# One attention-plus-mixture-of-experts kernel: VectorE work spread over more steps, with quotients and residual adds traced behind the next maxima

## The chip, the cores and the metric

The kernel runs on one core of one Trainium2 chip. The metric is the device time in microseconds (us) of one execution, and the time of a kernel is the median of its runs. Engines are called as in the profile: PE is the matrix engine (PEld its weight loads), DVE is VectorE, ACT is ScalarE, POOL is GpSimd, SP is SyncE, which issues most DMAs.

## The reference

The input x has 8 batches of 512 rows of 128 numbers. One layer is computed, all in float32:

```
x = x + attention(layernorm(x))      # 16 heads of 8 columns, causal, softmax(q k^T / sqrt(8)) v, then Wo, bo
x = x + experts(layernorm(x))        # 8 experts, the best 2 of each row by a softmax gate:
                                     # sum over 2 of p * (relu(x w1 + b1) w2 + b2), F = 512
```

## The kernel before, in words

**A score is computed twice.** For every head, `shifts()` multiplies q and k (tiles `s`, query rows on the partitions) only to find the maximum of each row; DVE reads each 128x512 bank of PSUM with a `tensor_reduce` (line 642, tile `pm`). The negated maxima (`nm`, line 648) are split into two bf16 numbers (`nh`), transposed by PE (`nmTp`, line 588), copied by ACT (`nmT`) and written by a POOL DMA into two extra rows of `q2` (line 596). `attend()` then multiplies k and q again with these rows (tiles `st`, key rows on the partitions, lines 783 and 788), ACT takes the exponential (line 793, tile `pt`), and PE accumulates the product with v in one PSUM bank `po` (line 704). The tiles `s` and `st` share one pool of four PSUM banks (`ps_sc`), so PE can start the next score only when DVE (for `s`) or ACT (for `st`) has read the bank of four tiles before.

**After two groups of four heads** ACT copies `po` to `ob` (line 713), and `divide()` transposes it on PE (`oqp`, line 725), then DVE takes a reciprocal (`rd`, line 728) and multiplies twice (`on`, line 730). After the last group of a batch, `out_T()` transposes `on` on PE (`oTp`, line 748), ACT copies it (`oT`, line 750), `out_project()` multiplies by Wo (`pp`, line 756), and DVE adds x (line 760).

**Then a batch is routed.** `route()` computes the second layer norm (`layernorm`, named f0 to f7), the gate, the two best experts of each row and a slot for each, all in small DVE instructions; `dispatch()` follows after batches 1, 3, 5, 6 and 7 and decides which tiles of 128 slots are complete. `scatter()` writes the rows to DRAM with 8 indirect DMAs of POOL for each batch (line 1052). `experts()` gathers them (SP DMAs, `xg<-xs`, line 1215), turns them (`xgTp`, line 1246; `xgT`, line 1248), multiplies with w1 (`ph`, line 1287), adds the bias and clips (`hT`: two of the four 128x128 pieces on ACT, line 1294, and two on DVE, line 1296; in the tail after batch 7, three and one), multiplies with w2 (`py`, line 1146), adds b2 on DVE (`yo`, line 1150) and writes the rows back with an indirect DMA (`ys`, line 1184). `sums()` adds the two results of each row at the end (line 1365).

**The order is written by hand.** Each of these parts is a generator that yields due times, in units of one batch of attention; the lane with the earliest due time traces its next instructions. PE, ACT, DVE and SP execute exactly in the order of tracing (`ORDERED`), and so do those instructions of POOL that go through `G_ops` or `in_order`. An instruction that waits therefore holds all that stands behind it on its engine. `in_order` also ties each indirect DMA to the exponential traced last before it. Steps of `attend()` are called in `go_on()`: one product and one waiting step (`late`) at each of 24 places in a batch. In `route()`, `soon(n)` moves the due time on by n steps of 0.012 to 0.025 batch.

The first layer norm of batch b (named a0 to a7) is traced in `norms()` for b of 2 and more: statistics (lines 369 and 370) on DVE from b - 2.16, a reciprocal root on POOL, and the normalised rows `xn` with four DVE instructions (line 384) from b - 2.0. `project()` transposes them at b - 1.84 (`xnTp_a`, line 395) and multiplies with Wv (`pv`, line 567) at b - 0.85.

Of the kernel before, what the change touches and what calls it, by code (L numbers as in the profile page):

```python
# [18 lines left out]
P = 128  # L19
# [7 lines left out]
def preln_attn_moe(ctx: ExitStack, tc: tile.TileContext, x, wq, wk, wv, wo, bo,  # L27
# [337 lines left out]
    def layernorm(src, name, t, each):  # L365
        stats = small.tile([P, NT, 6], F32, tag="stats", name=f"stats_{name}")
        mv = small.tile([P, NT, 2], F32, tag="mv", name=f"mv_{name}")
        for c in range(NT):
            nc.vector.bn_stats(stats[:, c, :], src[:, c, :])
            nc.vector.bn_aggr(mv[:, c, :], stats[:, c, :])  # L370
            yield t[0] + each * (c + 1)
        rstd = small.tile([P, NT], F32, tag="rstd", name=f"rstd_{name}")
        ve = small.tile([P, NT], F32, tag="ve", name=f"ve_{name}")
        first = name in ("a0", "a1")
        on_pool = nc.gpsimd if first else G_ops
        on_pool.tensor_tensor(ve, mv[:, :, 1], eps, ALU.add)
        on_pool.tensor_tensor(rstd, ve, mhalf, ALU.pow)
        yield t[1]
        xn = work.tile(
            [P, NT, D if name[0] == "a" else XROW], F32, tag=f"xn{name[0]}", name=f"xn_{name}",  # L380
            bufs=1 if name[0] == "a" else XB,
        )
        for c in range(NT):
            nc.vector.tensor_scalar(  # L384
                xn[:, c, :D], src[:, c, :], mv[:, c, 0:1], rstd[:, c : c + 1],
                ALU.subtract, ALU.mult,
            )
            if c < NT - 1:
                yield t[1] + each * (c + 1)
        return xn  # L390
# [11 lines left out]

    def norms():
        for b in range(2, B):
            yield b - 2.16
            normal[b] = yield from layernorm(xt[b], f"a{b}", (b - 2.16, b - 2.0), 0.025)


    packed, shifted, attended, added = set(), set(), set(), set()


    def project():
# [17 lines left out]
        for b in range(B):  # L430
# [7 lines left out]
                xn = normal.pop(b)  # L438
            if 0 < b < B - 2:
                xt[b + 2] = load_x(b + 2)  # L440
            yield b - (1.84 if b > 1 else 1.21 if b == 1 else 1.41)
            xnT = rows_T(xn, f"a{b}")
            late = 0.19 if b == 1 else 0.0
            yield b - (1.40 if early else 1.36) - early + late
# [115 lines left out]
                pack(0, 1)  # L560
                pack(1, 1)
            packed.add(b)
            yield b - 0.85
            assert b < 2 or b - 2 in added
            pv = mm_tile(f"pv_{b}")
            for c in range(NT):
# [16 lines left out]
    def shifts():  # L583
        late = []

        def transposed(b, g, nh):
            pt = mm_tile(f"nmTp_{b}_{g}").bitcast(BF16)
            nc.tensor.transpose(pt[:, :P], nh, ident_bf)
            nmT = small.tile([32, P], BF16, tag="nmT", name=f"nmT_{b}_{g}")
            nc.scalar.copy(nmT, pt[:32, :P])  # L590
            late.append(lambda: rows(b, g, nmT))

        def rows(b, g, nmT):

            for l in range(2):
                ins = nc.gpsimd.dma_start(  # L596
                    out=q2_buf[b % 2][KS + l : KS + l + 1, HG * g : HG * g + HG],
                    in_=nmT[16 * l : 16 * l + 16],
                )
                if b > 0:  # L600
                    tc.keep_in_program_order(ins)
            shifted.add((b, g, 2))

        for b in range(B):
            for g in range(G):
                t0 = b - LEAD + g / G + (0.1 if b == 0 < g else 0.0)
                yield t0
                assert b in packed
                q2, k2 = q2_buf[b % 2], k2_buf[b % 2]

                pm = pm_buf[g % 2].rearrange("p (n u) t k -> p u n (t k)", u=2)
                for pr in range(2):
                    n = 2 * g + pr
                    for i, unit in enumerate(S_UNITS):
                        yield t0 + (3 * pr + i) / 24
                        for v, bank in enumerate(unit):
                            ps = ps_sc.tile(
                                [P, T], F32, tag="sc", name=f"s_{b}_{n}_{i}_{v}"
                            )
                            for u, t, at in bank:  # L620
                                h, q = 2 * n + u, ts(t, P)
                                if t > 0:
                                    nc.tensor.matmul(  # L623
                                        ps[:, at : at + t * P], lhsT=q2[:KS, h, q],
                                        rhs=k2[:KS, h, : t * P],
                                        start=(at == 0), stop=True, skip_group_check=True,
                                    )
                                nc.tensor.matmul(  # L628
                                    ps[:, at + t * P : at + (t + 1) * P],
                                    lhsT=q2[:, h, q], rhs=k2[:, h, q],  # L630
                                    start=(at + t == 0), stop=True, skip_group_check=True,
                                )
                            blocks = ps.rearrange("p (a q) -> p a q", q=P)
                            if i == 0:
                                top, src = pm[:, v, pr, 12:13], ps
                            elif i == 1:
                                top, src = pm[:, v, pr, 3:7], blocks
                            else:
                                top, src = pm[:, :, pr, 8], ps.rearrange(
                                    "p (u k) -> p u k", u=2  # L640
                                )
                            nc.vector.tensor_reduce(top, src, AX.X, ALU.max)  # L642
                        if t0 + (3 * pr + i) / 24 < 0:
                            keep_warm(WARM[2], f"{g}_{pr}_{i}")
                        if late:
                            late.pop(0)()
                nm = small.tile([P, HG * NT], F32, tag="nm", name=f"nm_{b}_{g}")
                nc.vector.tensor_reduce(  # L648
                    nm, pm_buf[g % 2].rearrange("p h t k -> p (h t) k"), AX.X, ALU.max,
                    negate=True,  # L650
                )
                nh = nh_buf[g % 2]
                nm = nm.rearrange("p (h o a) -> p h o a", o=2, a=2)
                hi, lo = (
                    nh[:, ts(l, HG * NT)].rearrange("p (h a o) -> p h o a", a=2, o=2)
                    for l in range(2)
                )
                on_pool = V if b == 0 else G_ops
                on_pool.tensor_copy(hi, nm)
                on_pool.tensor_tensor(lo, nm, hi, ALU.subtract)  # L660
                if b > 0:
                    late.append(lambda: None)
                late.append(lambda b=b, g=g, nh=nh: transposed(b, g, nh))
                if b == 0 and g == 0:
                    for n in range(2):
                        yield t0 + (6 + n) / 24
                        late.pop(0)()
        while late:
            late.pop(0)()
            yield B - LEAD + 0.05  # L670


    def attend():
# [46 lines left out]
        def divide(b, ob, g):  # L720
# [4 lines left out]
                nc.tensor.transpose(pt[:, ts(t, P)], ob[:, ts(t, P)], ident)  # L725
            oq = pt.rearrange("p (k r) -> p k r", r=32)
            rd = small.tile([P, NT * HG, 2], F32, tag="rd", name=f"rd_{b}_{g}")
            nc.vector.reciprocal(rd, oq[:, :, HD : 2 * VC : VC])
            for o in range(2):
                nc.vector.tensor_tensor(  # L730
                    on[b][:, :, ts(g // 2, D // 2)].rearrange(
                        "p t (h o d) -> p t h o d", o=2, d=HD
                    )[:, :, :, o],
                    pt.rearrange("p (t h r) -> p t h r", t=NT, h=HG)[
                        :, :, :, VC * o : VC * o + HD
                    ],
                    rd[:, :, o].rearrange("p (t h) -> p t h", t=NT).unsqueeze(3).to_broadcast(
                        [P, NT, HG, HD]
                    ),
                    ALU.mult,  # L740
                )
            if g == G - 1:
                late.append(lambda: out_T(b))

# [8 lines left out]
        def out_project(b, oT):  # L753
            pp = mm_tile(f"pp_{b}")
            for t in range(NT):
# [1 line left out]
                    pp[:, ts(t, P)], lhsT=oT[:, ts(t, P)], rhs=wo_sb, start=True,  # L757
                    stop=True,
                )
            nc.vector.tensor_tensor(  # L760
                xt[b], pp.rearrange("p (c d) -> p c d", c=NT), xt[b], ALU.add
            )

        for b in range(B):
            for g in range(G):
# [46 lines left out]
    def route():  # L812
        for b in range(B):
# [8 lines left out]
                return now[0]  # L822

            yield now[0]
            t = [soon(0), soon(7), soon(4 if b == B - 1 else 6)]
            xn2[b] = yield from layernorm(
                xt[b], f"f{b}", t, step / 2 if b == B - 1 else step
            )
# [113 lines left out]
            lanes.append([now[0], 100 + b, scatter(k, b, now[0])])  # L942
            for s, (_, after, _, _) in enumerate(STEPS):
                if after == b:
                    yield from dispatch(s, soon)


    def dispatch(s, soon):
# [134 lines left out]
    def experts():  # L1083
# [192 lines left out]
        for n, (s, i) in enumerate(tiles):  # L1276
# [9 lines left out]
            for c in range(FC):  # L1286
# [1 line left out]
                    ph[:, ts(c, P)], lhsT=wt[s, i][:, ts(c, P)],  # L1288
                    rhs=turned[s, first][:, ts(i - first, P)], start=True, stop=True,
                )  # L1290
            for c in range(FC):
                bias = wt[s, i][:, F + c : F + c + 1]
                if c < (FC - 1 if after(s, i) else FC // 2):
                    nc.scalar.activation(hT[:, c, :], ph[:, ts(c, P)], AF.Relu, bias=bias)  # L1294
# [129 lines left out]
```

## Time and profile before

| what | value |
|---|---|
| time, median of 3 runs | 583.0 us (582.61 to 583.82) |
| the profiled execution's own time | 580.48 us |
| its span, first to last instruction | 578.8 us |
| mean granted TensorE clock | 0.966 |
| busy: PE, DVE, ACT, POOL | 506.7, 410.5, 307.3, 242.4 us |
| attention, 40 to 445 us: PE busy | 369.4 of 405 us |
| tail, 445 to 579 us: PE busy | 105.4 of 134 us |

The profiled execution is 2.5 us faster than the median of the runs, and 1.7 us of its time lie outside its span. Up to about 40 us the first batch is prepared; from there to about 445 us eight batches of attention follow at some 50.6 us each, and from 207 us on the experts' tiles run between them; then come the remaining tiles and the sums. A row of the waits reads: engine, tile and line that waited, who ended the wait, total us, number of times, longest us.

### The profile page before, as it was taken

What the parts mean: (1) busy time and instruction counts of PE and PEld (TensorE: products, weight loads), DVE (VectorE), ACT (ScalarE), POOL (GpSimd) and SP (SyncE); (2) the same over time, 40 slices, a digit from 0 to 9 for tenths busy, and PEclk for the clock granted to TensorE, in tenths of its full rate; (3) what the DMA queues carried; (4) which work ended last, traced back from release to release, by engine and by line L of the source; (5) the groups of instructions that cost most, each with busy time, mean ns of one, the idle gap of its engine ahead of it and who ended that gap; (6) DMA issues with size and microseconds to landing.
All of it is one profiled execution on the core that took longest, in us unless ns stands there. A gap on an engine that the chain in (4) does not pass through costs nothing. (4 is left out here: it accounts for less than half of the span.)

```text
span 578.8 us, 14044 instructions
## 1 busy us (share of the span) xinstructions
PE 506.7 (88%) x4762; PEld 373.9 (65%) x4762; DVE 410.5 (71%) x1272; ACT 307.3 (53%) x673; POOL 242.4 (42%) x380
## 2 busy tenths in 40 slices
PE   8868999988987989999899999998898889789980
PEld 6644556556544565665567777766576878689980
DVE  4987787887888779778978678787653445233694
ACT  3645666755754665575556555554564434245530
POOL 4032212405716423661753356345435524644442
PEclk9888899999998999999999999999999979989995
DMA  3728667288299572535526573222333686758783
GB/s 82 190 66 202 150 157 184 59 206 191 73 193 188 145 193 55 133 80 130 158 65 169 116 193 94 66 66 76 102 107 117 199 269 190 208 165 263 239 303 104
DMA packets 68761, 86.06 MB, mean 149 GB/s; under 512 B 11540, under 2 KB 50748, under 8 KB 66652
## 3 DMA queue, kind: packets, MB, share of 16 engines
q1 hardware_dynamic: 61508, 74.87, 50.0%
q0 software_dynamic: 6592, 9.65, 5.2%
q8 instruction: 39, 0.64, 0.5%
q10 hardware_dynamic: 592, 0.66, 0.5%
q14 instruction: 30, 0.25, 0.1%
HBM read 61.34 MB, written 26.16 MB: 151 GB/s over the span
## 5 line engine op out<-in xcount | busy, mean ns | idle before, releaser
L793 ACT ACTIVATE pt<-st 128x512 f32<-128x512 f32 x320 | 178.4, 599 | 109.0 <-PE st L783 49.3
L642 DVE TENSOR_REDUCE pm<-s 128x1 f32<-128x512 f32 (+2 forms) x320 | 205.5, 680 | 27.0 <-PE s L628 23.3
L1184 POOL DMA_INDIRECT ys<-yo,to x78 | 76.5, 980 | 99.1 <-ACT pt L793 32.4
L623 PE MATMUL s<-k,q 72*128 72x384 bf16 (+2 forms) x384 | 93.3, 278 | 15.8 <-ACT pt L793 9.9
L628 PE MATMUL s<-k,q 128*128 128x128 bf16 x512 | 94.1, 223 | 7.9 <-ACT pt L793 5.2
L783 PE MATMUL st<-q,k 128*128 128x128 bf16 x512 | 91.0, 220 | 10.2 <-DVE pm L642 5.5
L704 PE MATMUL po<-pt,va 128*18 128x512 f32 (+3 forms) x1024 | 91.6, 444 | 1.4 <-ACT pt L793 1.4
L788 PE MATMUL st<-q,k 74*128 74x256 bf16 (+2 forms) x384 | 91.9, 276 | 0.0
L1146 PE MATMUL py<-w_sb,hT 128*128 x624 | 87.4, 283 | 4.5 <-DVE have L962 2.2
L1146 PEld LDWEIGHTS py<-w_sb,hT 128*128 128x128 f32 x624 | 78.8, 197 | 7.8 <-issue 5.2
L1052 POOL DMA_INDIRECT xs<-xn_f,slot x64 | 64.0, 1000 | 30.9 <-ACT pt L793 15.6
L628 PEld LDWEIGHTS <-q 128*128 128x128 bf16 x512 | 50.9, 100 | 32.2 <-issue 29.2
L623 PEld LDWEIGHTS <-q 72*128 72x128 bf16 x384 | 37.6, 99 | 39.8 <-issue 32.2
L783 PEld LDWEIGHTS <-k 128*128 128x128 bf16 x512 | 50.9, 100 | 4.0
L788 PEld LDWEIGHTS <-k 74*128 74x128 bf16 x384 | 37.4, 98 | 22.7 <-issue 17.2
L596 POOL DMA_DIRECT2D q<-nmT x64 | 34.1, 536 | 39.5 <-ACT nmT L590 37.2
L358 POOL CAST nh<-nm 128x16 bf16<-128x16 f32 x28 | 5.6, 198 | 91.8 <-DVE nm L648 90.8
L1296 DVE TENSOR_SCALAR hT<-ph,wt 128x128 f32<-128x128 f32 x72 | 21.9, 346 | 28.8 <-ACT hT L1294 23.5
L704 PEld LDWEIGHTS po<-pt,va 128*18 128x18 f32 x1024 | 22.7, 96 | 30.1 <-issue 21.8
L1294 ACT ACTIVATE hT<-ph,wt 128x128 f32<-128x128 f32 x72 | 22.6, 364 | 35.7 <-issue 12.3
L1287 PE MATMUL ph<-xgT,wt 128*128 128x128 f32 x288 | 40.1, 282 | 0.7 <-issue 0.4
L1287 PEld LDWEIGHTS ph<-xgT,wt 128*128 128x128 f32 x288 | 35.0, 191 | 5.6 <-issue 2.7
(185 smaller groups left out, 697.6 us busy)
## 6 DMA issues: line engine op xcount, KB each, us to landing
wt<-wrows SPq DMA_DIRECT2D x36, 322.0 KB
k<-kparts SPq DMA_DIRECT2D x42, 192.0 KB
q<-wrows SPq DMA_DIRECT2D x24, 322.0 KB
k<-wrows SPq DMA_DIRECT2D x18, 322.0 KB
q<-qparts SPq DMA_DIRECT2D x30, 192.0 KB
q<-ys SPq DMA_DIRECT2D x15, 256.0 KB
k<-xs SPq DMA_DIRECT2D x42, 65.0 KB
qparts<-part SPq DMA_DIRECT2D x14, 192.0 KB
```

The source lines that it names most:

```text
L596: ins = nc.gpsimd.dma_start(out=q2_buf[b % 2][KS + l : KS + l + 1, HG * g : HG * g + HG], in_=nmT[16 * l : 16 * l + 16],)
L623: nc.tensor.matmul(ps[:, at : at + t * P], lhsT=q2[:KS, h, q], rhs=k2[:KS, h, : t * P], start=(at == 0), stop=True, skip_group_check=True,)
L628: nc.tensor.matmul(ps[:, at + t * P : at + (t + 1) * P], lhsT=q2[:, h, q], rhs=k2[:, h, q], start=(at + t == 0), stop=True, skip_group_che ...
L642: nc.vector.tensor_reduce(top, src, AX.X, ALU.max)
L704: nc.tensor.matmul(po[32 * h : 32 * h + 2 * VC, j * P :], lhsT=va[:, j, c0 : c0 + 2 * VC], rhs=at_cols(pts[pr], unit, u, at, W), start=(fi ...
L783: nc.tensor.matmul(ps[:, at : at + P], lhsT=k2[:, h, k], rhs=q2[:, h, k], start=(at == 0), stop=True, skip_group_check=True,)
L788: nc.tensor.matmul(ps[:, at + P : at + T - j * P], lhsT=k2[:KO, h, k], rhs=q2[:KO, h, (j + 1) * P :], start=False, stop=True, skip_group_c ...
L793: last_exp[0] = nc.scalar.activation(pt[:, v, :], ps, AF.Exp, scale=SCALE)
L1052: ins = nc.gpsimd.indirect_dma_start(out=xs[k], out_offset=bass.IndirectOffsetOnAxis(ap=slot[b][:, j * NT + i : j * NT + i + 1], axis=0), ...
L1146: nc.tensor.matmul(py, lhsT=hT[:, c, :], rhs=w2_sb[:, bass.ds(at[s, i] + c * E * D, D)], start=(c == 0), stop=(c == FC - 1),)
L1184: ins = nc.gpsimd.indirect_dma_start(out=ys[k], out_offset=bass.IndirectOffsetOnAxis(ap=to[s, first][:, i - first : i - first + 1], axis=0 ...
L1287: nc.tensor.matmul(ph[:, ts(c, P)], lhsT=wt[s, i][:, ts(c, P)], rhs=turned[s, first][:, ts(i - first, P)], start=True, stop=True,)
```

## The change

- `layernorm()` of a2 to a7: the four normalising instructions go from DVE to POOL (`tensor_scalar` with add of the negated mean and multiply), in POOL's fixed order, and one small POOL instruction negates the mean. The statistics of a3 to a7 are traced 0.34 batch earlier, at b - 2.5.
- `project()`: the transposes of `xn` move from b - 1.84 to b - 1.76, `pv` from b - 0.85 to b - 0.9.
- `divide()` and `out_project()`: for all batches but the last, the DVE part (reciprocal and two products; the add of x) is put in a list, which `shifts()` empties right after the maxima of its next unit are traced.
- `route()`: for b below 6 the normalised rows come 3 steps later, and with them all that follows; `dispatch()` after batches 1, 3 and 5 takes steps 1.8 times as long.
- `experts()`: the pieces of `hT` are traced from the last to the first, so DVE's come ahead of ACT's.

```diff
@@ layernorm
+        apart = name[0] == "a" and not first
+        if apart:
+            mean = small.tile([P, NT], F32, tag="mean", name=f"mean_{name}")
+            on_pool.tensor_scalar(mean, mv[:, :, 0], -1.0, 0.0, ALU.mult, ALU.add)
         for c in range(NT):
-            nc.vector.tensor_scalar(
-                xn[:, c, :D], src[:, c, :], mv[:, c, 0:1], rstd[:, c : c + 1],
-                ALU.subtract, ALU.mult,
-            )
+            if apart:
+                on_pool.tensor_scalar(
+                    xn[:, c, :D], src[:, c, :], mean[:, c : c + 1], rstd[:, c : c + 1],
+                    ALU.add, ALU.mult,
+                )
+            else:
+                nc.vector.tensor_scalar(
...
@@ norms
-            yield b - 2.16
-            normal[b] = yield from layernorm(xt[b], f"a{b}", (b - 2.16, b - 2.0), 0.025)
+            t = b - (2.16 if b == 2 else 2.5)
+            yield t
+            normal[b] = yield from layernorm(xt[b], f"a{b}", (t, t + 0.16), 0.025)
+    behind_maxima = []
@@ project
-            yield b - (1.84 if b > 1 else 1.21 if b == 1 else 1.41)
+            yield b - (1.76 if b > 1 else 1.21 if b == 1 else 1.41)
...
-            yield b - 0.85
+            yield b - (0.9 if b > 1 else 0.85)
@@ shifts
                             nc.vector.tensor_reduce(top, src, AX.X, ALU.max)
+                        while behind_maxima:
+                            behind_maxima.pop(0)()
@@ divide
-            nc.vector.reciprocal(rd, oq[:, :, HD : 2 * VC : VC])
-            for o in range(2):
-                nc.vector.tensor_tensor(
...
+            def scaled():
+                nc.vector.reciprocal(rd, oq[:, :, HD : 2 * VC : VC])
+                for o in range(2):
+                    nc.vector.tensor_tensor(
...
+            if b < B - 1:
+                behind_maxima.append(scaled)
+            else:
+                scaled()
             if g == G - 1:
                 late.append(lambda: out_T(b))
@@ out_project
+            def add():
+                nc.vector.tensor_tensor(
+                    xt[b], pp.rearrange("p (c d) -> p c d", c=NT), xt[b], ALU.add
+                )
+            if b < B - 1:
+                behind_maxima.append(add)
+            else:
+                add()
@@ route
-            t = [soon(0), soon(7), soon(4 if b == B - 1 else 6)]
+            t = [soon(0), soon(7 if b >= B - 2 else 10), soon(4 if b == B - 1 else 6)]
...
-                    yield from dispatch(s, soon)
+                    wide_steps = 1.0 if b >= B - 2 else 1.8
+                    yield from dispatch(s, lambda n=1.0: soon(n * wide_steps))
@@ experts
-            for c in range(FC):
+            for c in reversed(range(FC)):
                 bias = wt[s, i][:, F + c : F + c + 1]
                 if c < (FC - 1 if after(s, i) else FC // 2):
                     nc.scalar.activation(hT[:, c, :], ph[:, ts(c, P)], AF.Relu, bias=bias)
                 else:
                     nc.vector.tensor_scalar(
```

More of the change, by code (lines that the diff above doesn't have):

```diff
@@ L382, in layernorm @@
         )
+        apart = name[0] == "a" and not first
+        if apart:
+            mean = small.tile([P, NT], F32, tag="mean", name=f"mean_{name}")
+            on_pool.tensor_scalar(mean, mv[:, :, 0], -1.0, 0.0, ALU.mult, ALU.add)
         for c in range(NT):
-            nc.vector.tensor_scalar(
-                xn[:, c, :D], src[:, c, :], mv[:, c, 0:1], rstd[:, c : c + 1],
-                ALU.subtract, ALU.mult,
-            )
+            if apart:
[5 more added lines that the diff above has]
+                nc.vector.tensor_scalar(
+                    xn[:, c, :D], src[:, c, :], mv[:, c, 0:1], rstd[:, c : c + 1],
+                    ALU.subtract, ALU.mult,
+                )
             if c < NT - 1:
@@ L727, in divide @@
             rd = small.tile([P, NT * HG, 2], F32, tag="rd", name=f"rd_{b}_{g}")
-            nc.vector.reciprocal(rd, oq[:, :, HD : 2 * VC : VC])
-            for o in range(2):
[L730 to L741, printed above, removed]
+            def scaled():
+                nc.vector.reciprocal(rd, oq[:, :, HD : 2 * VC : VC])
+                for o in range(2):
+                    nc.vector.tensor_tensor(
+                        on[b][:, :, ts(g // 2, D // 2)].rearrange(
+                            "p t (h o d) -> p t h o d", o=2, d=HD
+                        )[:, :, :, o],
+                        pt.rearrange("p (t h r) -> p t h r", t=NT, h=HG)[
+                            :, :, :, VC * o : VC * o + HD
+                        ],
+                        rd[:, :, o].rearrange("p (t h) -> p t h", t=NT).unsqueeze(3).to_broadcast(
+                            [P, NT, HG, HD]
+                        ),
+                        ALU.mult,
+                    )
+            if b < B - 1:
+                behind_maxima.append(scaled)
+            else:
+                scaled()
             if g == G - 1:
@@ L759, in out_project @@
                 )
-            nc.vector.tensor_tensor(
-                xt[b], pp.rearrange("p (c d) -> p c d", c=NT), xt[b], ALU.add
-            )
+            def add():
+                nc.vector.tensor_tensor(
+                    xt[b], pp.rearrange("p (c d) -> p c d", c=NT), xt[b], ALU.add
+                )
+            if b < B - 1:
+                behind_maxima.append(add)
+            else:
+                add()
         for b in range(B):
```

## The prediction

> **What bounds the kernel now.** I read the page's busy shares first, then its slices.
>
> ```profile
> PE 506.7 (88%) x4762; PEld 373.9 (65%) x4762; DVE 410.5 (71%) x1272; ACT 307.3 (53%) x673; POOL 242.4 (42%) x380
> ```
>
> PE is the bound, with DVE behind it. A window of 40 to 445 us (the eight batches of attention) has PE busy 369.4 of 405 us, DVE 316.7, ACT 237.6 and POOL 171.7. An edit that leaves PE's work alone can only bring back PE's idle 35.6 us there. So the next view is PE's waits in that window:
>
> ```profile
> PE s L623 <- ACT pt L793: 9.9, 20, 1.5
> PE st L783 <- DVE pm L642: 5.5, 14, 2.2
> PE s L628 <- ACT pt L793: 5.2, 10, 0.6
> PE st L783 <- ACT pt L793: 2.3, 5, 0.7
> PE s L628 <- DVE pm L642: 2.2, 4, 0.8
> PE nmTp L588 <- DVE nh L660: 2.2, 2, 1.1
> PE s L623 <- DVE pm L642: 1.3, 2, 1.0
> ```
>
> Late maxima end 5.5 + 2.2 + 1.3 = 9.0 us of it, late `nh` 2.2, and late exponentials 9.9 + 5.2 + 2.3 = 17.4. That is what spreading DVE's work can win (11.2 and perhaps some of the 17.4). The third view is what DVE itself waits for, all engines, from 40 to 440 us:
>
> ```profile
> DVE hT L1296 <- ACT hT L1294: 14.8, 15, 2.1
> DVE rd L728 <- PE oqp L725: 12.2, 11, 1.6
> DVE x L760 <- PE pp L756: 10.6, 7, 1.8
> ```
>
> These three waits hold the maxima behind them and are what the deferral and the reversed `hT` remove. Whether that helps depends on who else needs the deferred work; the timeline at the end of batch 0's attention shows it:
>
> ```profile
> 92.72 0.66 PE L725 MATMUL oqp<-ident,ob 128*128 128x128 f32 x4
> ...
> 93.41 0.36 DVE L728 RECIPROCAL rd<-oqp 128x32 f32<-128x32 f32 x1 [0.93 <-PE oqp L725]
> ...
> 93.81 0.49 DVE L730 TENSOR_TENSOR on<-oqp,rd 128x128 f32<-128x128 f32 x2
> ...
> 94.21 1.28 DVE L642 TENSOR_REDUCE pm<-s 128x4 f32<-128x512 f32 x2
> 94.35 0.42 PEld L748 LDWEIGHTS oTp<-ident,on 128*128 128x128 f32 x4 [0.30 <-DVE on L730]
> 94.35 0.66 PE L748 MATMUL oTp<-ident,on 128*128 128x128 f32 x4
> ```
>
> PE comes to the transposes `oTp` 0.06 us after `on` is ready, and has waited 0.30 for it. That edge has no slack already.
>
> **The quotients behind the maxima (a loss).** In the changed order PE still has `oTp` in the same place, behind the next two scores, but DVE runs two maxima (1.28 us together) before `rd` (0.36) and `on` (0.49). In return DVE does not wait 0.93 us for `oqp`; but those scores stand behind `oqp` in PE's order, so the maxima can start only about 0.5 us earlier than `rd`, `on` and they do now (first bank full near 93.6 instead of 94.21). `on` then ends at about 95.70 instead of 94.29, and PE, which is at `oTp` at 94.35, waits 1.35 us. The same reckoning for the quotients at each batch's end, with the time of `oTp` of each: batch 0 1.35, batch 1 1.35 (140.00 against 138.65), batch 2 1.04 (188.48, 187.44), batch 3 1.59, batch 4 1.18, batch 5 0.64, batch 6 1.35: together 8.5 us. Batch 7 is not deferred. The other quotients of a batch (after two groups) feed nothing near. PE queues behind `oTp` all scores and values that follow, so the stall is on the path. Some comes back, since DVE and ACT catch up meanwhile and PE's later waits for them (28.6 us of the 405) shrink: I take a quarter off. Bounds 3 (half lost to earlier maxima, more catching up) and 8.5; taken **6.5**. The add of x behind two maxima costs nothing: its x is wanted by `route()` at the earliest some steps later. Its wait (10.6 us in all) goes, but the maxima behind it read scores that stand behind `pp` on PE: they started at 99.53 when the add ended then, and could by 0.25 to 0.85 us earlier. I book that under the gains.
>
> **`hT` reversed (a loss).** Now ACT clips two pieces at once when `ph` is done, then takes the next exponential, and DVE comes when it is free. One tile:
>
> ```profile
> 243.82 0.62 ACT L1294 ACTIVATE hT<-ph,wt 128x128 f32<-128x128 f32 x2 [0.69 <-PE ph L1287]
> ...
> 244.34 2.21 ACT L793 ACTIVATE pt<-st 128x512 f32<-128x512 f32 x4
> ...
> 244.84 0.61 DVE L1296 TENSOR_SCALAR hT<-ph,wt 128x128 f32<-128x128 f32 x2
> ```
>
> In the built order the first piece on DVE waits for PE alone, and ACT's first piece waits for DVE's. So ACT would start at 245.44 instead of 243.82, and the exponentials queued behind it 1.6 us later; the bank that PE needs next had 0.27 us of slack. Going through all 30 tiles from 207 to 440 us: on 17 DVE is prompt, and ACT waits about 0.6 us (0.31 a piece); on 13 DVE is behind maxima, and ACT waits 1.4 to 2.6 us. After the slack of the banks, PE's stalls add up to 12.4 us if DVE comes when it does now, and to about 5 if it comes 0.6 us earlier, which the 14.8 us of DVE's waits for ACT allow (15 waits of 1 us each, the maxima behind them earlier too). Bounds 0 and 12.4; taken **4.5**, near the lower reckoning because DVE is the engine that gets freed. In the tail there are no maxima, and PE is two tiles ahead: 0 (up to 2).
>
> **Routing spread (a loss of a later gather).** Three more steps of 0.018 batch are 0.054 x 50.6 = 2.7 us, and the last `scatter` of batches 1, 3 and 5 lands behind one more exponential and the q rows' DMAs (536 ns each): some 2.1 us later. Now batch 1's last scatter starts at 195.47, the gather's packets end at 201.87 and `xgTp` starts at 203.21; batch 3's end at 302.48 for a turn at 303.40; batch 5's at 417.83 for 418.13, though there other transfers fill the queue. So PE would wait 0.8 and 1.2 us at the first turns, and SP's queue stands longer at the gathers, with x, weights and q parts behind it (no row shows one wanted within 2 us). Bounds 0 and 4; taken **2**.
>
> **`xn` on POOL (hidden).** Six batches times four instructions of 348 ns leave DVE: 8.4 us. POOL has no such instruction now. Between its 128x128 row (284 ns) and a quarter of its add of 128x512 (1281 ns, 0.47 with a fixed part of 0.2 as its 128x4 rows have) four take 1.1 to 1.9 us, plus 0.2 for the mean. POOL is busy 42%, and its biggest waits are for ACT's `nmT` (29.4 us) and DVE's `nm` (90.8 us). Queued behind them in POOL's order are the q rows' DMAs of group 0, which would go about 1 us later and are read some 10 us later; PE wants the turned `xn` some 30 us after its trace. Taken 0, up to 2 if a score of group 0 is just in time. `pv` 0.05 batch earlier and `xnTp` 0.08 later only change places with scores: 0.
>
> The adds of x and bo on POOL run 1.27 to 1.30 us each among DVE's maxima, so no slowing shows between those two. [...]
>
> **The gains.** DVE's 9.0 + 2.2 us of PE's waits. The 8.4 us and the routing's small instructions, spread over more gaps, take perhaps half of the 9.0: 4.5. Of `rstd_f6`, which DVE waited 3.0 us for (`xn_f`, once) and PE 2.2 behind it, about 1.2. Some bursts only move: the statistics of the first norm now meet `xn_f` of an older batch, with 1.3 to 1.6 us between maxima. Bounds 2 and 12.3 (all of 9.0 + 2.2, and the rest of the maxima that start earlier); taken **5.7**.
>
> **Sum.** 6.5 + 4.5 + 2 + 0 - 5.7 = +7.3 us on the profiled 580.5: 587.8. The median of the runs shown is 2.5 us above that execution, so 590.3.
>
> **Rivals.**
>
> A. *Faster: the freed DVE decides.* All of the 11.2 us ended by DVE go, and with maxima never behind a wait some of the 17.4 ended by ACT (up to 6), while `on` comes in time. For it: DVE is at 78% in the attention and waits 37.6 us in the three rows shown. Against it: two maxima of 0.64 stand before `on` by the traced order, so PE must lose 1.28 somewhere else to be in time. The point from which it decides: `oTp` and `hT` together cost less than the gains, that is under 5 us. Time 583 - 11 to 583 - 2: 571 to 581, with the gathers at 0 to 2.
>
> B. *Slower by more: ACT behind DVE at full price.* If DVE comes to `hT` no earlier than now, 12.4 replaces 4.5, and `oTp` costs its 8.5: 580.5 + 8.5 + 12.4 + 2 - 5.7 = 597.7, and 600.2 as a median. It decides where DVE, whose maxima run without a break, has no gap left when `ph` ends. 597 to 606.
>
> C. *The change pays for itself.* Stalls of PE are caught up at the next waits (oTp 3, hT 2, gathers 1 against 5.7): within 3 us of the time before, 580 to 585.
>
> **How the numbers follow.** My sum, 585 to 597: 0.50. A 0.22, B 0.13, C 0.15. A measurement of this kernel can tell some 0.2%, 1.2 us, from no change. Of C, 0.07 lie within that, 0.03 below and 0.05 above. So faster 0.22 + 0.03 = 0.25, same 0.07, slower 0.50 + 0.13 + 0.05 = 0.68. The likeliest case's own range is 585 to 597; with half of A and half of B beyond the ends, 576 to 601 leaves out about 0.18.
>
> **What would show it.** Right: waits of `oTp` for `on` go from 2.0 us (6 times) to some 8, seven times about 1.2; waits of ACT's `hT` for DVE's appear, 20 to 35 us, and those of DVE's `hT` for ACT's are gone; waits of scores for the maxima fall from 9.0 to about 4, and those for exponentials rise above 17.4; the first `xgTp` after a gather waits about 1 us. The rows of `rd` for `oqp` and x for `pp` vanish in any case. Wrong: `oTp` waits under 3 us (the maxima start much earlier than I reckon), or ACT's waits at `hT` that no score feels, or PE's busy time in 40 to 445 us spread over fewer than 405 us; then A is right. Four normalising instructions of over 2.5 us on POOL would void my zero there.

## The result, and the profile after

The changed kernel took 615.69 us (median of 4 runs, 613.08 to 619.01) beside 583.41 us of the kernel before: ratio 1.0556, 95% interval 1.0502 to 1.061. The forecast's direction was right, its size was not: +32 us, where +7.3 and at most 601 us were forecast. All ratios here are of runs within 1.5% of the fastest of their kernel. The profiled execution has a span of 617.3 us, 38.5 more than before. From its page:

```profile
PE 526.6 (85%) x4762; PEld 383.4 (62%) x4762; DVE 410.6 (67%) x1248; ACT 305.0 (49%) x673; POOL 253.5 (41%) x410
PEclk9977879999999989997898999899999998989996
```

The first reading is one that I had not made before: PE ran the same 4762 instructions and was busy 19.9 us longer for them (526.6 against 506.7). They were not more work; they ran at a lower clock (mean granted clock 0.941 against 0.966). The row PEclk has a 7 or an 8 in 11 of its 40 slices, where before it has one in 7. The rest of the 38.5 us, 18.6, is PE idle. PE's waits from 40 to 485 us name most of that:

```profile
PE st L811 <- DVE pm L655: 11.3, 18, 2.0
PE oTp L770 <- DVE on L747: 9.5, 7, 1.5
PE s L636 <- DVE pm L655: 5.2, 9, 1.6
PE st L811 <- DMA q<-nmT: 3.6, 2, 2.6
PE st L811 <- ACT pt L821: 3.3, 4, 1.9
PE xgTp L1275 <- DMA xg<-xs: 2.8, 6, 0.8
PE s L636 <- ACT pt L821: 2.4, 6, 0.8
...
PE s L641 <- DVE pm L655: 1.6, 4, 0.8
...
PE s L641 <- ACT pt L821: 1.0, 2, 0.5
```

Three rows are new (that of `oTp` had 0.3 us before), and all three were named in the prediction: `oTp` waits for `on`, q for its rows from `nmT`, `xgTp` for the gather. Waits for maxima, which the change was to shorten, doubled: 11.3 + 5.2 + 1.6 = 18.1 us against 9.0. Waits for exponentials, which the prediction saw rise above 17.4, fell to 3.3 + 2.4 + 1.0 = 6.7. At the end of batch 0 the deferral looks as reckoned:

```profile
103.09 1.29 DVE L655 TENSOR_REDUCE pm<-s 128x4 f32<-128x512 f32 x2 [2.37 <-PE s L641]
104.29 0.35 DVE L745 RECIPROCAL rd<-oqp 128x32 f32<-128x32 f32 x1
104.67 0.49 DVE L747 TENSOR_TENSOR on<-oqp,rd 128x128 f32<-128x128 f32 x2
105.22 0.42 PEld L770 LDWEIGHTS oTp<-ident,on 128*128 128x128 f32 x4 [1.72 <-DVE on L747]
105.22 0.66 PE L770 MATMUL oTp<-ident,on 128*128 128x128 f32 x4 [1.50 <-DVE on L747]
```

And this is one of the experts' tiles, from the timeline:

```profile
384.32 0.61 DVE L1326 TENSOR_SCALAR hT<-ph,wt 128x128 f32<-128x128 f32 x2
384.85 1.28 DVE L655 TENSOR_REDUCE pm<-s 128x1 f32<-128x512 f32 x2
385.11 0.62 ACT L1324 ACTIVATE hT<-ph,wt 128x128 f32<-128x128 f32 x2 [3.20 <-DVE hT L1326]
385.62 1.73 ACT L821 ACTIVATE pt<-st 128x512 f32<-128x512 f32 x3
386.27 0.22 PE L811 MATMUL st<-q,k 128*128 128x128 bf16 x1 [1.85 <-ACT pt L821]
```

ACT stood 3.20 us at `hT`: 0.9 for `ph`, which ended at 382.81, and 2.3 for DVE, which had one more maximum and five small instructions of the second norm ahead of its own pieces. Three exponentials queued behind it, and PE lost 1.85 us for a bank. Windows of 2 us show what came next (the window's length first, then PE busy; PEclk is third from the end):

```profile
384.00:386.00 2.00, 0.38 (x2) 0.19 (x2) 1.97 (x6) 0.89 (x3) 1.48 (x3) 1.00 0.04 10
386.00:388.00 2.00, 1.73 (x14) 0.50 (x13) 0.13 (x1) 1.79 (x4) 1.00 (x1) 0.85 0.00 0
388.00:390.00 2.00, 2.00 (x12) 1.81 (x9) 0.00 (x0) 0.00 (x0) 1.09 (x2) 0.50 0.17 52
390.00:392.00 2.00, 2.00 (x22) 1.78 (x19) 1.58 (x3) 0.52 (x2) 0.97 (x1) 0.80 0.30 55
```

Read in windows of 0.05 us, the granted clock is 0.50 from 387.4 to 390.8 us, for 3.4 us, behind 3.4 us in which PE was busy 1.5. What sets it no run shows. (1 - PEclk) x PE busy, summed over windows of 1 us, gives 29.4 us lost to the clock after and 13.2 before: each 3.4 us in which PE had work cost 1.4 to 1.7 us, and some stretches last 6.8 us.

### The profile page after: what moved, and what is told of

Same layout as the page of the kernel before. It is cut to its first block, busy times and chain, and to the rows that moved or that the text cites. A ratio compares the mean times of both kernels' runs of the same rounds, so it can differ in the third digit from the quotient of the medians.

```text
span 617.3 us, 14072 instructions
## 1 busy us (share of the span) xinstructions
PE 526.6 (85%) x4762; PEld 383.4 (62%) x4762; DVE 410.6 (67%) x1248; ACT 305.0 (49%) x673; POOL 253.5 (41%) x410
## 4 chain that ended last, share of the span: by engine, by line
PE 46%; DVE 23%; DMA 10%; issue 9%; ACT 5%; POOL 4%; SPq 2%; DVEq 0%; POOLq 0%; ACTq 0%; another core or an unknown queue 0%
DVE pm L655 10%; PE po L719 10%; PE py L1175 6%; PE ph L1316 6%; PE s L636 4%; PE st L816 4%; PE st L811 3%; DMA q<-nmT 3%; PE s L641 3%; DVE hT L1326 2%; DMA xs<-xn_f,slot 2%; ACT pt L821 2%; PE pq L481 2%; DVE x L1395 2%; ACT hT L1324 1%
## 5 line engine op out<-in xcount | busy, mean ns | idle before, releaser
L811 PE MATMUL st<-q,k 128*128 128x128 bf16 x512 | 93.3, 225 | 20.6 <-DVE pm L655 11.3
L636 PE MATMUL s<-k,q 72*128 72x384 bf16 (+2 forms) x384 | 96.3, 285 | 14.2 <-DVE pm L655 6.7
L641 PE MATMUL s<-k,q 128*128 128x128 bf16 x512 | 95.5, 227 | 3.5 <-DVE pm L655 1.8
L719 PE MATMUL po<-pt,va 128*18 128x512 f32 (+3 forms) x1024 | 97.4, 461 | 1.1 <-ACT pt L821 1.1
L816 PE MATMUL st<-q,k 74*128 74x256 bf16 (+2 forms) x384 | 95.2, 284 | 0.0
L1175 PE MATMUL py<-w_sb,hT 128*128 x624 | 89.8, 290 | 4.5 <-ACT hT L1324 3.0
L1175 PEld LDWEIGHTS py<-w_sb,hT 128*128 128x128 f32 x624 | 81.0, 202 | 8.6 <-ACT hT L1324 3.7
L811 PEld LDWEIGHTS <-k 128*128 128x128 bf16 x512 | 52.4, 103 | 8.3 <-issue 3.1
L816 PEld LDWEIGHTS <-k 74*128 74x128 bf16 x384 | 38.4, 100 | 29.6 <-issue 23.6
L719 PEld LDWEIGHTS po<-pt,va 128*18 128x18 f32 x1024 | 24.9, 98 | 31.0 <-issue 21.4
```

What stands on the lines that cost most here:

```text
L636: nc.tensor.matmul(ps[:, at : at + t * P], lhsT=q2[:KS, h, q], rhs=k2[:KS, h, : t * P], start=(at == 0), stop=True, skip_group_check=True,)
L641: nc.tensor.matmul(ps[:, at + t * P : at + (t + 1) * P], lhsT=q2[:, h, q], rhs=k2[:, h, q], start=(at + t == 0), stop=True, skip_group_che ...
L719: nc.tensor.matmul(po[32 * h : 32 * h + 2 * VC, j * P :], lhsT=va[:, j, c0 : c0 + 2 * VC], rhs=at_cols(pts[pr], unit, u, at, W), start=(fi ...
L811: nc.tensor.matmul(ps[:, at : at + P], lhsT=k2[:, h, k], rhs=q2[:, h, k], start=(at == 0), stop=True, skip_group_check=True,)
L816: nc.tensor.matmul(ps[:, at + P : at + T - j * P], lhsT=k2[:KO, h, k], rhs=q2[:KO, h, (j + 1) * P :], start=False, stop=True, skip_group_c ...
L1175: nc.tensor.matmul(py, lhsT=hT[:, c, :], rhs=w2_sb[:, bass.ds(at[s, i] + c * E * D, D)], start=(c == 0), stop=(c == FC - 1),)
```

## The experiments

Ratios are to runs of the kernel before on the same chip, with their 95% intervals. (Chips differ: the kernel before took 583 to 585 us on some and 565 to 567 us on others.) "Clock" is the mean granted TensorE clock over the runs, that of the kernel named first, then that of before.

### One part undone

`u_defer`: `scaled()` and `add()` called at once. `u_hT`: `reversed` taken out. `u_norm`: `apart = False`, and the old due times. `u_route`: `soon(7)`, `wide_steps = 1.0`.

> The changed kernel with the quotients and the add of x traced at once again, as before. Theory (each part costs by the stalls that it makes on PE, and the half-clock stretches after long stalls are shared out among them): the waits of oTp for on, 9.5 us in seven batches, go, and no half-clock stretch follows one of them directly, so some 9 us come back: 606. Rival 1 (one part alone carries the loss, the normalising on POOL): under 3 us come back, 613 to 616. Rival 2 (the deferral carries most): over 20 us come back, under 596.

> The changed kernel with the pieces of hT in their old order, ACT's ahead of DVE's. Theory: ACT's 24.6 us of waits for DVE at hT go, and with them about half of the waits of scores for maxima and exponentials that grew (DVE-ended 9.0 to 18.1 us) and two or three half-clock stretches of 1.7 us: 10 us come back, 606. Rival 1 (POOL alone): under 3 us. Rival 2 (ACT behind DVE at its full price, as in my prediction's rival B): 12 to 17 us, 599 to 604.

> The changed kernel with the first layer norm as before: normalised on DVE, statistics, turns and pv at their old times. Theory: the q rows' DMAs of group 0 go out ahead of the add of x and bo on POOL again, so the 2.6 us wait of st for q at 59.6 us goes, and with it the half-clock stretches at 59 to 67 and 76 to 84 us (3.3 and 3.4 us lost): about 11 us come back, 605, nearly all of it before 100 us. Rival 1 (this part carries the whole loss): over 20 us. [...]

> The changed kernel with the routing and dispatch at their old steps. Theory: the gathers come 2 to 3 us earlier, and the waits of xgTp for its gather (2.8 us) go, so 2 to 4 us come back: 612 to 614. Rival (the spread routing was worth something to DVE): 0 to 5 us slower than the changed kernel.

| undone | ratio to before | what came back of 5.56% |
|---|---|---|
| deferral | 1.032 (1.025 to 1.039) | 2.4% |
| reversed hT | 1.0204 (1.010 to 1.0309) | 3.5% |
| normalising on POOL | 1.0465 (1.0383 to 1.0546) | 0.9% |
| routing spread | 1.0297 (1.0191 to 1.0403) | 2.6% |

No part carries the loss alone. The deferral did what its theory said (604.4 us, 606 expected). The reversed `hT` gave back more, as its rival 2 had it (599.9, the middle of the three runs that its ratio rests on). The POOL part, where I had looked for 11 us, is the smallest (612.5), and the routing gave back more than the 2.8 us that `xgTp` waits: 607.6 is the median of its four runs (599 to 610), and its ratio rests on the two faster ones. In sum 9.4% came back of 5.56%, so undoing single parts does not divide the loss.

### One part alone

> The kernel before with only the quotients and the add of x traced behind the maxima. Theory (the parts add up; undoing this one gave 11 of 32 us): oTp waits for on 1.5 us in each of six batches, no half-clock stretch follows them directly, 9 to 11 us slower than before. Rival (the parts cost only together, because each alone leaves slack to the other): at most 4 us slower.

> The kernel before with only the pieces of hT traced from the last to the first. Theory (undoing gave 15 us): ACT waits for DVE at hT for 40 to 70 us in all, late exponentials and maxima make PE idle, and there are two or three more half-clock stretches: 10 to 15 us slower. Rival (cost only together): at most 5 us slower, my prediction's 4.5.

> The kernel before with only the first layer norm changed: normalised on POOL, statistics earlier, turns later, pv earlier. Theory (undoing gave 3 us, no more than runs of one kernel differ): 0 to 4 us slower, the add of x and bo going ahead of the first q rows' DMAs on POOL. Rival 1 (it frees DVE, as the change says): 3 to 8 us faster. Rival 2 (the half-clock stretches at 59 to 67 and 76 to 84 us come with it): 6 to 12 us slower.

> The kernel before with only the routing and dispatch spread over more steps. Theory (undoing gave 8 us): later gathers make the first xgTp wait, and the routing's bursts meet other DVE work: 2 to 8 us slower. Rival 1 (spreading helps DVE when nothing else is in its way): 1 to 5 us faster. Rival 2 (nothing by itself): within 1.5 us of before.

| alone | ratio to before | us (565.5 before) | clock, this and before |
|---|---|---|---|
| deferral | 1.0138 (1.0052 to 1.0223) | +7.8 | 0.963, 0.962 |
| reversed hT | 1.0259 (1.0178 to 1.034) | +14.6 | 0.964, 0.962 |
| normalising on POOL | 0.9921 (0.9881 to 0.996) | -3.4 | 0.961, 0.962 |
| routing spread | 1.0083 (1.0031 to 1.0135) | +5.2 | 0.961, 0.962 |

Alone, each part costs or gains without a change of the clock beyond 0.002. The deferral has its wait nearly whole in the view of the tile `oTp` (rows of PE and PEld together, 14 waits for seven batches):

```profile
  DVE on L747: 20.6, 14
```

The reversed `hT` and the routing cost what their theories said, the deferral a little less (9 to 11 us expected), and the normalising goes to its rival 1, that it frees DVE, as the change says. The sum of the four is 24.2 us; each has an interval of 2 to 5 us to either side, and the sum one of about 8.

### Together, on one chip

> The kernel before itself, for its trace beside the others of this call: within 1% of the other runs of before on this chip. It settles whether a part alone (its half-clock stretches lost 11.5 to 19.8 us) has any more of them than before has on the same chip; theory: before loses 11 to 14 us.

> The changed kernel itself, for its ratio beside its parts. The parts alone gave +1.4, +2.6, -0.8 and +0.8%, in sum +4.0%. Theory (stalls of several parts in one stretch of 3 or 4 us bring the clock to half, which none does alone): 5.0 to 5.8% slower here too, and 10 us or more of clock lost beyond what before loses. Rival (the parts add up, and the rest was another chip's): 3.5 to 4.3% slower, clock lost as before.

> The kernel before with two parts, the reversed hT and the deferral behind the maxima; normalising and routing as before. Alone they gave +2.6 and +1.4%. Theory (half-clock stretches come from both together): 4.5 to 5.5% slower, clock lost 6 us or more beyond before's. Rival (they add up): 3.6 to 4.3%.

> The kernel before with the first layer norm on POOL as in the change, but for batches 3 to 7 alone: that of batch 2 is normalised on DVE as before, so that the add of x and bo stays behind the first q rows' DMAs on POOL. With all batches it was 0.8% faster, though it lost some 6 us before 94 us against before (exponentials 20 and 40 ended at 70.6 and 94.1 instead of 66.4 and 88.3). Theory: these 4 to 6 us come back: 1.4 to 1.9% faster than before. [...]

`n37` is the kernel before with `apart = name[0] == "a" and int(name[1:]) > 2` and the change's due times in `norms()` and `project()`.

| kernel | ratio to before | clock, this and before |
|---|---|---|
| the change | 1.0511 (1.0411 to 1.0611) | 0.946, 0.963 |
| hT and deferral | 1.0505 (1.0417 to 1.0594) | 0.945, 0.963 |
| normalising of 3 to 7 on POOL | 1.0003 (0.9961 to 1.0045) | 0.954, 0.963 |

The two parts make nearly the whole loss; the other two nearly cancel, as they did alone (-3.4 and +5.2 us). The records lose 19.7 us to the clock in before here (more than the 11 to 14 expected), 26.3 with the two parts and 29.6 with all; the record of before is one of its slower runs (clock 0.952, the mean is 0.963). And the mean clock over the runs falls by 0.017, as with no part alone. What that is worth can be read from runs of one and the same kernel: 19 runs of the kernel before on one chip go from 562.8 us at a clock of 0.971 to 571.2 us at 0.948, and the line through them falls 3.4 us for 0.01; ten on this chip give 3.4 too. By it, 0.017 are 5.9 us of the 31.6 us between the means of the change and of before here. It is less than the clock's loss in the records (29.6 us against 19.7); that ACT and DVE catch up while PE is slow would explain it, but was not shown. 24.2 + 5.9 = 30.1, which fits the reading that the parts add up and the clock is the rest. It is not proved: the intervals of both kernels, and that of the sum, are wide enough for plain addition too (their rivals' 4.3% lies inside), and no run held the clock fixed. What is measured is that the clock fell.

`n37` missed its theory. PE's wait for q's rows was gone and the early loss was not: exponential 40 ended at 91.1 us (88.6 in before here), behind half-clock stretches at 46 to 53 and 70 to 77 us that before has for half as long. That such stretches can differ where the work is the same, the last kernels show more sharply below.

### What each loss hangs on

`hT_late` traces the reversed pieces apart:

```diff
+                if c == FC // 2 - 1 and not after(s, i):
+                    yield when(s, i + 1.3)
```

`d_late` gives `on` the time that two maxima take:

```diff
             if g == G - 1:
+                if b < B - 1:
+                    late.append(lambda: None)
                 late.append(lambda: out_T(b))
```

`o_disp` keeps `wide_steps` and undoes the three steps of `route()`; `best1` is `d_late` with the normalising on POOL.

> The kernel before with the reversed hT, but in the attention ACT's two pieces are traced 0.3 of a tile later than DVE's, behind some four exponentials. Theory (the reversed order costs because ACT stands waiting for DVE with exponentials queued behind it): ACT's waits for DVE at hT fall from 72 to under 15 us, and of the 2.6% that the reversed order alone cost, at most 1.0% is left. Rival 1 (it costs because hT itself comes late to PE, or ph's bank is held longer): 2.5% or more. Rival 2 (it costs in the tail): 2% or more, with the attention as long as before's.

> The kernel before with the deferral behind the maxima, but out_T of batches 0 to 6 one step of go_on later, some 2 us. Theory (the deferral costs by oTp's wait for on, 1.49 us in each of six batches, and by nothing else, while DVE's waits for oqp and pp are gone): oTp waits under 1 us in all, and the time is 0.2 to 1.0% below before's. Rival 1 (the deferral also costs by rd and on behind two maxima in other ways): still 0.8% or more slower. Rival 2 (no gain was to be had from those waits): within 0.2%.

> The kernel before with dispatch after batches 1, 3 and 5 spread 1.8 times, and route() at its old steps. Together they cost 0.8%. Theory (the later gathers cost; dispatch alone doesn't move the rows' last scatter, which stands in its own lane): 0 to 0.3% slower. Rival (dispatch's end decides when a gather may go, so that the whole cost is its): 0.6 to 1.0% slower.

> The kernel before with the first layer norm of the change and the deferral with out_T one step later; hT and routing as before. Theory (at an equal clock normalising on POOL gave 0.8% and the harmless deferral gives 0.2 to 1.0%): 1.0 to 1.8% faster than before. [...]

| kernel | ratio to before | clock, this and before |
|---|---|---|
| hT_late | 0.9951 (0.9902 to 1.0000) | 0.970, 0.964 |
| d_late | 0.9882 (0.9810 to 0.9954) | 0.961, 0.964 |
| o_disp | 0.9952 (0.9909 to 0.9994) | 0.966, 0.964 |
| best1 | 0.9891 (0.9817 to 0.9965) | 0.961, 0.964 |

**hT.** The reversed order with ACT's pieces later costs nothing (0.5% faster than before). ACT's waits for DVE from 200 to 455 us, with the reversed order alone and then with ACT later:

```profile
ACT hT L1318 <- DVE hT L1320: 23.4, 12, 3.2
```

```profile
ACT hT L1320 <- DVE hT L1322: 10.8, 8, 3.2
```

The total of the span fell less than I expected (72 to 51 us instead of under 15), because some 40 us lie in the tail, where they cost nothing visible. The two kernels are 0.8 us apart at the 160th exponential, about 227 us, and at the last, the 320th, `hT_late` is 12.5 us ahead (442.9 against 455.4, on two chips; some 3 us of it are lost to the clock). PE's stalls over 0.9 us between are six of 8.8 us together with the reversed order and one of 1.58 us without the queue; the last of the six, 1.71 us, is that same one. Five of the six end with a late maximum and only one with a late exponential, so the waits alone do not name the queue; what does is the time of `hT_late`, which only traces ACT's two pieces, and with them the product with w2, behind those exponentials. So it is ACT that stands waiting with exponentials queued behind it; the tail is no main cause, since `hT_late` has the same reversed tail and costs nothing (between these two executions 6.0 us of 18.5 lie there, 3.4 of them lost to the clock), nor is `hT` late on PE, as here it is later still.

**Deferral.** With time for two maxima the deferral is a gain, of 1.2% where 0.2 to 1.0% was expected. In `d_late` and `best1` one statistic of each of batches 0 to 6 reads x without the add; `f_late` below has it behind the add.

**Routing.** Dispatch alone costs nothing (0.5% faster), so the 0.8% belong to the three steps in `route()`, or to both together. `xgTp` waited 2.1 us for its gather with both and 0.5 with dispatch alone, and 3.5 us more were lost to the clock (19.8 against 16.3). In `o_route` PE stood 2.47 us up to 419.77, and the clock was at half from 421.6 to 431.8 us; these windows show its first part. The score was late because a maximum stood on DVE behind batch 6's `xn_f`, which waited 3.25 us for `rstd_f` of POOL. That wait is in the kernel before as well (3.0 us, with PE's stall of 2.21 at 413.58) and in `o_disp` (3.05 and 2.22), with no half clock behind it in the first and 3.4 us of it in the second. So the stall is not the routing's; the clock behind it differs.

```profile
420.00:424.00 4.00, 3.79 (x34) 1.87 (x32) 3.10 (x8) 2.32 (x4) 1.53 (x4) 0.70 0.29 81
424.00:428.00 4.00, 4.00 (x25) 3.36 (x29) 1.12 (x6) 1.71 (x5) 0.72 (x2) 0.50 0.71 177
```

**best1.** Normalising on POOL added nothing to the repaired deferral: its 1.1% lies in its theory's 1.0 to 1.8%, but only by the deferral's share (1.2% alone).

### A version that beats both

> The kernel before with the deferral, out_T of batches 0 to 6 one step later, and the routing's first statistics 0.018 batch later, so that all four read x after the add. (In d_late and best1 the first of four statistics of each of batches 0 to 6 was traced ahead of the add and read x without it; the rest of the work was the same.) Theory (that one statistic of 0.28 us did not make d_late fast): 0.8 to 1.6% faster than before, oTp's wait for on under 1 us in all. Rival (it did, as it let the routing start before the add): within 0.4% of before or slower.

> As f_late, and the reversed hT with ACT's two pieces 0.3 of a tile later. Theory (the two take away different waits of DVE): 1.4 to 2.2% faster than before. Rival (both give DVE time that it has no use for twice): no faster than f_late.

```diff
-            now = [b + (1.24 if b < B - 1 else 1.14)]
+            now = [b + (1.258 if b < B - 1 else 1.14)]
-            t = [soon(0), soon(7), soon(4 if b == B - 1 else 6)]
+            t = [soon(0), soon(7 - (0.018 / step if b < B - 1 else 0)), soon(4 if b == B - 1 else 6)]
```

`f_late`: 0.9924 (0.9889 to 0.9958). `f_best`: 0.9882 (0.9831 to 0.9933), 559.8 us beside 567.2. So the statistic ahead of the add was not what made `d_late` fast, though its gain is just under what was expected; and the two repairs together are 1.2% faster than the kernel before, a little less than the theory's 1.4. Their intervals overlap, but on this one chip the mean of `f_best` is 2.9 us under that of `f_late` (six runs and twelve, spread by about 2 us), which speaks against the rival. In `f_late` the tile `oTp` waits for `on` no more (the engines' idle time before it now starts with these two rows, and none is for `on`), and DVE's waits that the change was meant to remove are nearly gone:

```profile
  PE oTp L772: 5.4, 7
  ACT pt L823: 1.1, 5
```

```profile
DVE rd L745 <- PE oqp L740: 0.8, 1, 0.8
DVE x L785 <- PE pp L780: 0.8, 1, 0.8
```

## Why the prediction was right and wrong

**Quotients behind the maxima: the mechanism right, the net by some luck.** 8.5 us of stalls were forecast, 1.35 at batch 0; 9.5 and 1.50 came, six of 1.5 us and one shorter. 6.5 net was taken, 7.8 measured alone. `f_late` splits it, on another chip: without the stall the deferral gains 4.3 us, so the stall costs about 12 us against that. The prediction took a quarter off the stall, and the 12.2 and 10.6 us of DVE's waits were worth something after all, which it doubted; the two errors nearly cancel.

**Reversed hT: the mechanism right, the term mis-sized.** "Taken 4.5, near the lower reckoning because DVE is the engine that gets freed" is the step that failed: alone it cost 14.6 us, beyond the 12.4 that I gave as its upper end. DVE was not there 0.6 us earlier; at 384 us it had a maximum and five small instructions ahead of its pieces. At that tile ACT stood 2.3 us for DVE, as the upper reckoning had it where DVE is behind maxima (1.4 to 2.6 us). The price was that of rival B, to which I gave 0.13, and B's range still stops at 606.

**A term that was not in the sum: the clock.** Every stall was priced at its own length. The page of before had the row PEclk with 8s and a 7 in it, and its windows would have shown 0.50 behind PE's stalls at 42 to 47 us:

```profile
PEclk9888899999998999999999999999999979989995
...
44.00:46.00 2.00, 1.00 (x7) 0.44 (x5) 1.93 (x6) 1.19 (x2) 0.93 (x1) 1.00 0.91 240
46.00:48.00 2.00, 1.44 (x12) 1.00 (x13) 1.97 (x7) 1.29 (x3) 0.74 (x2) 0.86 0.92 261
48.00:50.00 2.00, 2.00 (x16) 0.73 (x13) 1.47 (x4) 1.10 (x3) 1.65 (x2) 0.50 0.85 214
```

I took off a quarter of the stalls for catching up, where a charge for the clock had the larger size: some 6 us over the runs, 16 in the records of the two executions.

**Routing: 2 us taken, 5.2 measured alone**, though the wait it was priced by is as forecast (2.1 us alone, 2.8 in the change). What else it costs is open.

**xn on POOL: right as an instruction, wrong as nothing.** Four take 1.74 us (1.1 to 1.9 forecast). But they stand with the add of x and bo ahead of batch 0's first q rows: that DMA went at 48.79 us instead of 47.26, and a score waited 2.62 us for it at 59.63. "Read some 10 us later" was the distance in before, and no proof of slack. **Gains: 5.7 taken**; the normalising alone gave 3.4, and in company nothing that can be measured. Waits for maxima, which were to fall from 9.0 to about 4 us, rose to 18.1 in the change, and the 3.0 us that `xn_f` waited for `rstd_f6`, of which 1.2 was booked, were 3.5.

The sum by measured terms is 7.8 + 14.6 + 5.2 - 3.4 = 24.2, plus 5.9 worked out for the clock: 30.1 of the 31.6 us. It failed first by `hT` (10 us), then by the clock (6), the routing (3) and the gains (2). The 0.2% that I took for what a measurement of this kernel can tell was too small as well: on one chip its runs before go from 562.8 to 571.2 us.

## What to carry to other kernels

When two engines share a step in a fixed order, ask which of them has the long queue behind it and let that one go first; the engine with the backlog goes last. A consumer with 0.06 us of slack must move together with the work that it needs: deferring the quotients lost 1.4% with `oTp` in place, and won 0.8% with `oTp` one step later. And where a trace shows half clock behind stalls that lie close together, charge them twice: once for themselves, and once for the slow clock behind them, here 1.4 to 1.7 us for each 3.4 us of it.

## What the runs showed of the hardware

In each of the 20 profiled executions the half-clock stretches begin on a grid. Read in windows of 0.05 us, the 14 of the changed kernel begin at 32.40, 46.05, 59.71, 76.77, 182.59 us and so on up to 605.84, all on one grid with steps of 3.413 us, to within 0.05 us. The eight of the kernel before lie on such a grid too, shifted by 1.4 us, and so do those of the 18 other runs, read in windows of 1 us, to within 0.07 us, with phases from 0.03 to 3.32 us. Counted by these steps, between 40 and 580 us, the 12 stretches that begin there in the changed kernel each follow a step in which PE was busy 0.8 to 2.15 of the 3.4 us; none follows a full stop of that length. The eight steps with the least work, up to 1.73 us, were each followed by one, but of the twelve with 1.78 to 2.15 only four were, so the busy time of the profile alone does not tell which are. The six stalls of 1.5 us at `oTp` were not followed by one: the four steps that hold such a stall whole still have 1.91 or 1.92 us of work, and the two stalls that fall across two steps leave 2.18 us or more in each.

`f_late` and `f_best` differ only in the experts' tiles, from 200 us on, and yet one had half-clock stretches at 46 to 50 us and the other at 46 to 53 and 69 to 77, and their 40th exponentials ended at 86.6 and 91.0 us. Their grids are 0.5 us apart. Apart from the last of each run, the stretches last 3.4, 6.8 or 10.2 us at 0.50, one to three steps of the grid. What decides whether one begins was not shown.

The normalising instruction took 437 to 452 ns on POOL in all 24 cases, next to a mean of 348 ns on DVE before: within 15 ns of each other, they show no slowing by what DVE did meanwhile.
